# Two-layer graph network: P4 and P5 of each projection made of seven quarter products, inner products first, their weights read from DRAM

## The chip, the core and the metric

The kernel runs on one core of a Trainium2 chip. The metric is the device time of one execution in microseconds; the time before is the median of three runs. The engines are PE (TensorE), DVE (VectorE), ACT (ScalarE), POOL (GpSimd) and SP (SyncE); here SP issues all DMAs.

## The reference

The input x holds 128 graphs of 128 nodes with 512 features, in float32; adj is one 128 x 128 mask. Two layers follow each other, and all products are float32.

```
# layer 0
q, k, v = x @ Wq.T, x @ Wk.T, x @ Wv.T
rel = adj.T * (q @ k.T);  rel = rel / norm(rel, axis=2)
x = layernorm(x + rel @ v)
# layer 1, 8 heads of 64
q, k, v = x @ Wq + bq, x @ Wk + bk, x @ Wv + bv
w = softmax(q @ k.T / 8 + mask(adj))       # per head
x = layernorm(x + (w @ v).merge_heads())
```

## The kernel before

Four graphs make a group g (512 tokens), and there are 32 groups (NG). Layer 0's q and k are folded: M = Wq^T Wk is computed once, and scores are x M x^T. So a group needs five projections of 512 tokens by a 512 x 512 weight: m and v0 of layer 0, and q, k and v1 of layer 1. v0 and v1 come out with tokens on partitions (`wide`), the others with features.

**Seven products.** A projection is a 2 x 2 block product done with seven half-size products instead of eight (Winograd's form of Strassen's method). Product i (P1 to P7) is 256 features by 256 tokens by 256 features: `product(i, bank)` makes it of four matmuls with a moving operand of 256 columns. P1, P6, P7 and P4 add up in one PSUM bank `a` (pool `ps_a`, two banks), which other engines read after each of them. Weight sums are made once (`weight_sums`, kept in `wc`), token sums for each group (`token_sums`, tile `tx`: t0 to t3). In the kernel before, P2 and P3 are not made whole: each is made of seven quarter products of 128 x 128 x 128 (`inner_product`, `inner(o, n)`), with inner weight sums (`wd` and parts of `wc`) and inner token sums (`inner_token_sums`, tile `ux`), in a bank `pc` of the pool `ps_m` (six banks). P1, P5, P6, P7 and P4 are whole. In group 0, m and v0 are `plain`: seven whole products. So is v1 in the last group.

**Order.** The order of all instructions is written out by hand: `at(r, k, f, ...)` puts a step at key 35 r + k, and the kernel emits the steps in order of their keys. Round r holds five projections: m and v0 of group r + 1 at keys 0 and 7, q, k and v1 of group r at 14, 21 and 28. Steps of a projection have keys 0 to 9.74 after its start, so that neighbours interleave. Between them stand the short steps, with keys from the tables ZERO, STEADY, QUICK and LAST. A key of 49 in STEADY means 14 in the next round. Each engine works through its own instructions in this order.

The short steps that matter here, for a group g and a graph b of it:

- `l0_score`: four matmuls, VectorE multiplies with adj (rel), POOL squares it (sq, L500). `l0_norm`: PE sums all four squares (pn, L509), VectorE transposes, POOL takes the power. `l0_out`: one matmul, then three VectorE instructions (L545, L518, L519).
- `attn_scores`: 8 matmuls into two banks, then VectorE's eight masks (L129). `attn_exp`: ScalarE's exponentials in pairs (L583). `attn_spill`, `attn_stage`, `attn_transpose`: the weights go through DRAM, and VectorE transposes them (wT, L602). `attn_out`: 8 matmuls (L615), a VectorE transpose (L618) and a reciprocal. `attn_sum`: one product on VectorE (L644), two sums on POOL (L646, L648). `attn_stats`: VectorE's statistics and four small POOL instructions.
- `x_transpose` and `x1_transpose`: four VectorE transposes for the input of layer 0 and of layer 1; the first half (dh 0) is followed by the token sum t0, the second by t1 (VectorE) and t2, t3 (POOL, L242, L243). Before the change, each transpose of dh 1 is followed by four inner token sums of 128 columns on POOL (L254 to L257).
- `restore`: two POOL copies that put back a weight for the plain v1.

Of the kernel before, what the change touches and what calls it, by code (L numbers as in the profile page):

```python
# [18 lines left out]
def kernel(  # L19
# [29 lines left out]
    small = ctx.enter_context(tc.tile_pool(name="small", bufs=4))  # L49
    dram = ctx.enter_context(tc.tile_pool(name="dram", bufs=2, space=bass.MemoryType.DRAM))  # L50
# [88 lines left out]
    wc = {n: const.tile([P, 7, 2, HF], F32, name=f"wc_{n}") for n in ("m", "v0", "q", "k", "v1")}  # L139


    wd = {n: const.tile([P, 2, 3, P], F32, name=f"wd_{n}") for n in wc}

    def inner_weight(key, o, i):
        if i >= 5:
            return wd[key][:, o - 2, i - 5]
        e, d = {1: (0, 0), 2: (0, 1), 3: (1, 0), 4: (1, 1)}[i]
        return wc[key][:, o - 1, d, e * P:(e + 1) * P]

    kept = const.tile([P, 2, P], F32, name="kept")  # L150

    def restore(key):

        for o in (2, 3):
            nc.gpsimd.tensor_copy(inner_weight(key, o, 3), kept[:, o - 2])

    def inner_weight_sums(key, eng):
        for o in (2, 3):
            w = [None] + [inner_weight(key, o, i) for i in range(1, 8)]
            if key == "v1":  # L160
                eng.tensor_copy(kept[:, o - 2], w[3])
            eng.tensor_tensor(w[5], w[3], w[4], op=ALU.add)
            eng.tensor_tensor(w[6], w[5], w[1], op=ALU.subtract)
            eng.tensor_tensor(w[7], w[1], w[3], op=ALU.subtract)
            eng.tensor_tensor(w[3], w[2], w[6], op=ALU.subtract)

    def weight_sums(t, a21, eng):
        eng.tensor_tensor(t[:, 4], a21, t[:, 3], op=ALU.add)
        eng.tensor_tensor(t[:, 5], t[:, 4], t[:, 0], op=ALU.subtract)
        eng.tensor_tensor(t[:, 6], t[:, 0], a21, op=ALU.subtract)  # L170
        eng.tensor_tensor(t[:, 2], t[:, 1], t[:, 5], op=ALU.subtract)

    def place(t, a21, dc, e, src, copy):

        if dc >= 2:
            dst = t[:, 3 if e else 1, dc - 2]
        else:
            dst = a21[:, dc] if e else t[:, 0, dc]
        copy(dst, src)
# [5 lines left out]

    m21 = two.tile([P, 2, HF], F32, tag="wT", name="m21")
    v21 = two.tile([P, 2, HF], F32, tag="wT", name="v21")

    def layer0_weights():
# [6 lines left out]
        wq_p = one.tile([P, C, C, A, Q], F32, tag="v1", name="wq0_p")  # L196
        for ec in range(C):
            copy = nc.scalar.copy if ec % 2 else nc.vector.tensor_copy
            copy(wq_p[:, ec], quadrants(wq_s[:, ec]))
        for h in range(2):  # L200
            for dh in range(2):
                dst = wc["v0"][:, 3 if h else 1] if dh else v21 if h else wc["v0"][:, 0]
                nc.vector.transpose(dst.rearrange("p c (t s) -> p c t s", s=Q),
                                    wv_s[:, h, :, :, 2 * dh:2 * dh + 2, :].rearrange("p b a c r -> p c (b a) r"))
        x_transpose(0, 0, 0)
        weight_sums(wc["v0"], v21, nc.vector)
        p = [ps_a.tile([P, D], F32, tag="a", name=f"pM_{dc}") if dc < 2 else
             ps_m.tile([P, D], F32, tag="m", name=f"pM_{dc}") for dc in range(C)]
        for ec in range(C):
            for dc in range(C):  # L210
                nc.tensor.matmul(p[dc], wq_p[:, ec, dc].rearrange("p q r -> p (q r)"), quadrants(wk_s[:, ec]),
                                 start=(ec == 0), stop=(ec == C - 1))
        for dc in range(C):
            for e in range(2):
                place(wc["m"], m21, dc, e, p[dc][:, e * HF:(e + 1) * HF], nc.scalar.copy)

    def layer1_weights(name, key):
        w, t = raw[name], wc[key]
        nc.gpsimd.tensor_copy(t[:, 0], w[:, 0:2, 0:HF])
        nc.gpsimd.tensor_copy(t[:, 1], w[:, 2:4, 0:HF])  # L220
        nc.gpsimd.tensor_copy(t[:, 3], w[:, 2:4, HF:D])
        weight_sums(t, w[:, 0:2, HF:D], nc.gpsimd)
# [13 lines left out]
    def token_sums(t, xT, dh, eng=nc.gpsimd):  # L236
# [3 lines left out]
        else:  # L240
            nc.vector.tensor_tensor(t[:, 1], quarter(xT, 1, 1), t[:, 0], op=ALU.subtract)
            nc.gpsimd.tensor_tensor(t[:, 2], quarter(xT, 1, 1), quarter(xT, 0, 1), op=ALU.subtract)  # L242
            nc.gpsimd.tensor_tensor(t[:, 3], quarter(xT, 1, 0), t[:, 1], op=ALU.subtract)  # L243

    def inner_token(xT, o, i):
        d, t = {1: (0, 0), 2: (1, 0), 3: (1, 1), 5: (0, 1)}[i]
        return xT[:, 2 + d, 2 * (o - 2) + t, :]

    def inner_token_sums(u, xT, o):

        b = {i: inner_token(xT, o, i) for i in (1, 2, 3, 5)}
        u = u[:, o - 2]
        eng = nc.gpsimd
        eng.tensor_tensor(u[:, 0], b[5], b[1], op=ALU.subtract)  # L254
        eng.tensor_tensor(u[:, 1], b[3], u[:, 0], op=ALU.subtract)
        eng.tensor_tensor(u[:, 2], b[3], b[5], op=ALU.subtract)
        eng.tensor_tensor(u[:, 3], b[2], u[:, 1], op=ALU.subtract)  # L257

    def x_transpose(g, dh, h):
# [5 lines left out]
        if dh == 1 and h == 0 and g:  # L265
            UX[g] = one.tile([P, 2, 4, P], F32, tag="ux", name=f"ux_{g}")
        transpose_quarter(XT[g], g, h, dh)
        if dh == 1 and g:
            inner_token_sums(UX[g], XT[g], 2 + h)
        if h:  # L270
            token_sums(TX[g], XT[g], dh, nc.gpsimd if g > 1 else nc.vector)
# [11 lines left out]
    def x1_transpose(g, dh, h):  # L283
# [4 lines left out]
        if dh == 1 and h == 0:  # L288
            UX1[g] = one.tile([P, 2, 4, P], F32, tag="ux1" if g < NG - 1 else "ux", name=f"ux1_{g}")
        transpose_quarter(X1T[g], g, h, dh)  # L290
        if dh == 1:
            inner_token_sums(UX1[g], X1T[g], 2 + h)
        if h:
            token_sums(TX1[g], X1T[g], dh)
# [6 lines left out]
    def shared(r):  # L301

        if r not in SX:
            t = one.tile([P, 2, 2, D], F32, tag="yT", name=f"sx_{r}")
            SX[r] = t[:, 0], t[:, 1].rearrange("p s (m e) -> p s m e", m=2)
# [4 lines left out]
    def room(g, b, of):  # L310

        if g >= NG - 2 or (g == NG - 3 and b >= 2):

            i = 2 * b + of if g == NG - 2 else 6 + 2 * b + of
            t = wc["m" if i < 7 else "v0"].rearrange("p i k e -> p (i k e)")
            return t[:, i % 7 * D:(i % 7 + 1) * D]
        if b < 2 and of:
            return shared(g + 1)[0][:, b]
# [8 lines left out]
    class Projection:  # L327


        def __init__(self, kind, g):  # L330
            self.kind, self.g = kind, g
            self.name = f"{kind}_{g}"
            self.w = wc[kind]
            self.wide = kind in ("v0", "v1")

        def begin(self):
            k, g = self.kind, self.g
            x0 = k in ("m", "v0")
            self.xT, self.t = (XT[g], TX[g]) if x0 else (X1T[g], TX1[g])

            self.plain = (x0 and g == 0) or (k == "v1" and g == NG - 1)

            self.late = k == "v1" and g < NG - 1
            if self.late:
                self.s0 = one.tile([P, 2, HF], F32, tag="rel", name=f"s0_{self.name}")
            else:
                self.place()
                self.s0 = self.out(0, 0)

        def place(self):  # L350
            k, g = self.kind, self.g
            if k == "m":
                YT[g] = self.y = one.tile([P, C, G, P], F32, tag="yT", name=f"yT_{g}")
            elif k == "q":
                QT[g] = self.y = one.tile([P, C, G, P], F32, tag="qT" if g < NG - 1 else "yT", name=f"qT_{g}")
            elif k == "k":
                KT[g] = self.y = one.tile([P, C, G, P], F32, tag="kT", name=f"kT_{g}")
            elif k == "v0":
                V0[g] = self.y = one.tile([P, G, D], F32, tag="v0", name=f"v0_{g}")
            else:  # L360
                V1[g] = self.y = one.tile([P, G, D], F32, tag="v1" if g < NG - 1 else "v0", name=f"v1_{g}")

        def out(self, eh, th):
            if self.wide:
                return self.y[:, 2 * th:2 * th + 2, eh * HF:(eh + 1) * HF]
            return quarter(self.y, eh, th)

        def product(self, i, bank, start, within=None):
# [3 lines left out]
            w_ = self.w[:, i - 1]  # L372
            for m in range(2):
                for k in range(2):
# [4 lines left out]
                    if within and m == 0 and k == 0:  # L379
                        within()  # L380

        def empty(self, dst, bank, eh):

            k = self.kind
            if k in ("m", "v0", "v1"):
                nc.scalar.copy(dst, bank)  # L386
            else:
                for m in range(2):
                    nc.scalar.activation(dst[:, m], bank[:, m], AF.Identity,  # L389
                                         bias=b1[k][:, 2 * eh + m:2 * eh + m + 1])  # L390

        def middle(self):

            if self.late:
                s = shared(self.g)[1]
                return s[:, 0], s[:, 1]
            return self.out(0, 1), self.out(1, 1)

        def quarters(self, o, j):

            e, t = j
            y = self.y.rearrange("p a b -> p (a b)" if self.wide else "p c b n -> p (c b n)")
            y = y.rearrange("p (j n) -> p j n", n=P)
# [505 lines left out]
```

## Time and profile before

| | before |
|---|---|
| median of 3 runs | 2438.91 us (2437.82 to 2439.96) |
| profiled execution, its span | 2436.5 us |
| granted TensorE clock, mean | 0.997 |
| PE busy, matmul records | 99%, 16548 |
| DVE, ACT, POOL busy | 76%, 41%, 47% |
| DMA queue of SP | 402.08 MB, 58.9% of 16 engines' span |

The times are those of whole executions, and the span lies between the first and the last instruction of one profiled execution, so a sum of durations is made against the span. A matmul in float32 shows as two records. Busy shares are sums of durations that may overlap by a little when instructions are pipelined. Norm matmuls (pn) of neighbouring groups start at 1266.7 and 1341.0 us, so a round of 35 keys takes 74.3 us and a key about 2.1 us.

### The profile page before, as it was taken

To read this page: it belongs to the slowest core of one execution; us is meant where nothing else is said; L and a number is where in the kernel's file an instruction comes from. 1 tells how busy PE (TensorE), PEld (TensorE's weight loads), DVE (VectorE), ACT (ScalarE), POOL (GpSimd) and SP (SyncE) were. 2 spreads that over 40 slices of the span, in tenths; PEclk is the share of its full clock that TensorE was granted. 3 is DMA by queue.
4 is the path that set the end of the run, shared out by engine and by line. 5 is a ranking of instruction groups with operands and counts; after the bars stand their busy time and mean duration, and the time that the engine had idled before them with its cause. 6 is when DMAs were issued, how large, how long until landed. Compare 5 with 4: busy or idle time off the path is not lost.

```text
span 2436.5 us, 49785 instructions
## 1 busy us (share of the span) xinstructions
PE 2417.1 (99%) x16548; PEld 2131.9 (87%) x16548; DVE 1863.8 (76%) x5934; ACT 1008.7 (41%) x3222; POOL 1138.8 (47%) x1792
## 2 busy tenths in 40 slices
PE   9999999999999999999999999999999999999998
PEld 6888888889888888888898888888888988888886
DVE  5667877777778778777777787787777777877877
ACT  1334343444444343534444443435344444434355
POOL 4624544435535355444455353554444553535543
PEclk9999999999999999999999999999999999999998
DMA  7356556566665665565666556655656665566454
GB/s 161 107 140 175 163 168 183 157 174 169 174 177 160 174 174 165 167 184 156 174 169 175 176 163 171 174 165 167 184 157 173 168 178 175 161 172 175 146 163 138
DMA packets 508611, 405.26 MB, mean 166 GB/s; under 512 B 37568, under 2 KB 424768, under 8 KB 508352
## 3 DMA queue, kind: packets, MB, share of 16 engines
q1 hardware_dynamic: 508352, 402.08, 58.9%
q8 instruction: 129, 2.11, 0.4%
q14 instruction: 130, 1.06, 0.2%
HBM read 237.31 MB, written 164.63 MB: 165 GB/s over the span
## 4 chain that ended last, share of the span: by engine, by line
PE 97%; DVE 1%; DMA 1%; ACT 0%; POOL 0%; issue 0%; SPq 0%; POOLq 0%; DVEq 0%; ACTq 0%
PE pa_v L376 18%; PE pa_q L376 9%; PE pa_m L376 9%; PE pa_k L376 9%; PE pc_v L419 8%; PE ps L563 5%; PE po L615 5%; PE pst L498 5%; PE pb_v L376 5%; PE po L543 4%; PE pc_k L419 4%; PE pc_q L419 4%; PE pc_m L419 4%; PE pb_k L376 2%; PE pb_q L376 2%; PE pb_m L376 2%
## 5 line engine op out<-in xcount | busy, mean ns | idle before, releaser
L523 POOL TENSOR_SCALAR ve<-st 128x1 f32<-128x1 f32 (+1 forms) x157 | 55.8, 356 | 749.2 <-DVE st L519 740.1
L583 ACT ACTIVATE w<-w,nmax 128x128 f32<-128x128 f32 x992 | 384.7, 401 | 4.6 <-DVE nmax L129 4.6
L376 PE MATMUL pa_v<-wc_v,tx 128*128 128x256 f32 x1536 | 368.8, 380 | 0.0
L376 PEld LDWEIGHTS pa_v<-wc_v,tx 128*128 128x128 f32 x1536 | 274.9, 191 | 29.0 <-issue 0.4
L129 DVE CUSTOM_DVE_ANT_0 w<-ps,mask 128x128 f32<-128x128 f32 x1024 | 221.8, 286 | 17.3 <-PE ps L563 15.7
L538 ACT ACTIVATE xr<-xr,sh,rstd 128x512 f32<-128x512 f32 x58 | 47.3, 815 | 401.7 <-POOL sh L533 401.7
L583 ACT ACTIVATION_READ_ACCUMULATOR w<-w,nmax 128x1 f32 x992 | 197.8, 199 | 0.0
L376 PE MATMUL pa_m<-tx,wc_m 128*128 128x256 f32 x768 | 183.8, 382 | 0.9 <-DVE yT L485 0.9
L425 DVE TENSOR_TENSOR v<-pc_v,v 128x256 f32<-128x256 f32 (+1 forms) x434 | 132.0, 309 | 68.4 <-PE pc_v L419 56.7
L376 PEld LDWEIGHTS pa_q<-tx,wc_q 128*128 128x128 f32 x768 | 143.2, 190 | 44.2 <-issue 28.9
L376 PE MATMUL pa_k<-tx,wc_k 128*128 128x256 f32 x768 | 181.8, 380 | 0.0
L376 PE MATMUL pa_q<-tx,wc_q 128*128 128x256 f32 x768 | 181.6, 379 | 0.0
L602 DVE STREAM_TRANSPOSE wT<-wl 128x1024 f32<-128x1024 f32 x124 | 153.4, 1237 | 3.3 <-DMA wl<-wd 3.0
L376 PEld LDWEIGHTS pa_m<-tx,wc_m 128*128 128x128 f32 x768 | 138.6, 190 | 16.4 <-DVE yT L485 1.3
L376 PEld LDWEIGHTS pa_k<-tx,wc_k 128*128 128x128 f32 x768 | 138.4, 190 | 14.9
L425 DVE TENSOR_TENSOR qT<-pc_q,qT 128x128 f32<-128x128 f32 (+1 forms) x320 | 98.4, 315 | 56.9 <-PE pc_q L419 48.4
L389 ACT ACTIVATE qT<-pa_q,bq_sb 128x256 f32<-128x256 f32 x128 | 53.7, 471 | 211.3 <-PE pa_q L376 199.4
L386 ACT COPY yT<-pa_m 128x512 f32<-128x512 f32 x64 | 37.5, 587 | 245.0 <-DVE v L425 112.1
L419 PE MATMUL pc_v<-wd_v,ux 128*128 128x128 f32 x744 | 133.3, 274 | 0.0
L646 POOL TENSOR_TENSOR xr<-xr,bv_b 128x512 f32<-128x512 f32 x58 | 73.8, 1273 | 124.8 <-DMA xr<-x1d 94.8
L563 PE MATMUL ps<-kT,qT 64*128 64x128 f32 x1984 | 130.0, 279 | 0.8 <-DVE nmax L129 0.8
L543 PE MATMUL po<-v,rel 128*128 128x512 f32 x256 | 130.5, 593 | 0.0
(239 smaller groups left out, 6177.8 us busy)
## 6 DMA issues: line engine op xcount, KB each, us to landing
wd<-w SPq DMA_DIRECT2D x248, 256.0 KB, 3.0
wl<-wd SPq DMA_DIRECT2D x496, 128.0 KB, 2.9
xl_x<-in_x_dram SPq DMA_DIRECT2D x256, 128.0 KB, 5.9
x<-in_x_dram SPq DMA_DIRECT2D x64, 512.0 KB, 4.8
x1d<-x SPq DMA_DIRECT2D x64, 512.0 KB, 3.6
xl_h<-x1d SPq DMA_DIRECT2D x256, 128.0 KB, 2.8
od<-oT SPq DMA_DIRECT2D x496, 64.0 KB, 2.1
o<-od SPq DMA_DIRECT2D x118, 256.0 KB, 2.9
```

Source lines behind the costliest of these rows:

```text
L129: nc.vector.tensor_tensor_reduce(out=dst, in0=scores, in1=m, scale=-HD ** -0.5, scalar=3.0e38, op0=ALU.add, op1=ALU.min, accum_out=least)
L376: nc.tensor.matmul(bank[:, m, :], l[:, k, m * P:(m + 1) * P], r[:, k, :], start=start and m == 0 and k == 0, stop=(m == 1 and k == 1), ski ...
L419: nc.tensor.matmul(self.c[o][:, slot, :], l, r, start=start, stop=True, skip_group_check=True)
L425: nc.vector.tensor_tensor(y, self.c[o][:, slot], s if kept else y, op=ALU.add)
L498: nc.tensor.matmul(p, XT[g][:, dc, b, :], YT[g][:, dc, b, :], start=(dc == 0), stop=(dc == C - 1))
L523: nc.gpsimd.tensor_scalar(ve[:, :n], stats[:, :n, 1], EPS, None, op0=ALU.add)
L543: nc.tensor.matmul(p, REL[g][0][:, b, :], V0[g][:, b, :], start=True, stop=True)
L563: nc.tensor.matmul(p[s][:, :, a, :], QT[g][r, a, b, :], KT[g][r, a, b, :], start=True, stop=True)
L583: nc.scalar.activation(w[:, s, :, a, :], w[:, s, :, a, :], AF.Exp, bias=nmax[:, i:i + 1], scale=-1.0, accum_out=sums[:, i:i + 1])
L602: nc.vector.transpose(wT, SOFT[g, b][0].rearrange("p a i r -> p i a r"))
L615: nc.tensor.matmul(p[s * HD:(s + 1) * HD, a, :], V1[g][:, b, h * HD:(h + 1) * HD], wT[:, s * (H // 2) + a].rearrange("p q t -> p (q t)"), ...
L646: nc.gpsimd.tensor_tensor(xr, xr, bv_b, op=ALU.add)
```

## The change

P4 and P5 of every projection that isn't plain are now made of seven quarter products as well, so only P1, P6 and P7 are whole. v1 of the last group is no longer plain, and `restore` is gone.

- **Inner products.** `inner(th, n)` makes two inner projections at once: P2 with P4 for th = 0, P3 with P5 for th = 1. Each pair of matmuls writes neighbouring parts of one bank. For n = 0 to 2 it issues four matmuls of 128 columns, for n = 3 two. ScalarE copies the partial results out of the bank after n = 0 (one copy), n = 1 (two) and n = 3 (one); VectorE adds after n = 0 and n = 2. After n = 3 of th = 1 a new POOL instruction adds P3's and P5's parts (512 columns).
- **Whole products.** `whole(i, m)` makes half of a whole product (two matmuls); VectorE adds the bank to the output after each half of P1 and P6, and twice after P7. The bias of q and k is added there, by `scalar_tensor_tensor`.
- **Order.** Inner steps come first: keys 0 to 3.5 for th = 0, 2.4 to 5.83 for th = 1; the halves of P1, P6 and P7 at 4.17, 5.33, 6.5, 7.67, 8.83 and 10.0. Some keys of the tables move by up to 1.5 (32 to 32.75 for attn_scores, 10.5 to 11.5 for l0_score and so on).
- **Token sums.** The inner sums run on two blocks at a time (256 columns), all after the last transpose: t1 (VectorE), t3 (POOL), four sums of raw tokens, four of summed tokens, then t2. `ux` grows from 8 to 14 blocks.
- **Weights.** The parts for P4 and P5 (`WDR`, 7 KB a partition) are written to DRAM once, and `stream(kind, g)` reads them into a ring of two buffers for each projection, 7.5 keys before its start.

```diff
-    wc = {n: const.tile([P, 7, 2, HF], F32, name=f"wc_{n}") for n in ("m", "v0", "q", "k", "v1")}
+    wc = {n: const.tile([P, 5, 2, HF], F32, name=f"wc_{n}") for n in KINDS}
+    def stream(key, g):
+        WR[key, g] = ring.tile([P, 2, 7, P], F32, tag="wr", name=f"wr_{key}_{g}")
+        nc.sync.dma_start(WR[key, g], WDR[key])
...
+    def token_sums(t, xT, u, dh, eng=nc.gpsimd):
         if dh == 0:
             eng.tensor_tensor(t[:, 0], quarter(xT, 0, 1), quarter(xT, 0, 0), op=ALU.subtract)
-        else:
-            nc.vector.tensor_tensor(t[:, 1], quarter(xT, 1, 1), t[:, 0], op=ALU.subtract)
-            nc.gpsimd.tensor_tensor(t[:, 2], quarter(xT, 1, 1), quarter(xT, 0, 1), op=ALU.subtract)
-            nc.gpsimd.tensor_tensor(t[:, 3], quarter(xT, 1, 0), t[:, 1], op=ALU.subtract)
+            return
+        nc.vector.tensor_tensor(t[:, 1], quarter(xT, 1, 1), t[:, 0], op=ALU.subtract)
+        nc.gpsimd.tensor_tensor(t[:, 3], quarter(xT, 1, 0), t[:, 1], op=ALU.subtract)
+        if u is not None:
+            inner_token_sums([None] + [raw_token(xT, i) for i in (1, 2, 3)] + [None, raw_token(xT, 5)],
+                             [u[:, j:j + 5:4] for j in range(4)])
+            r = [None] + [sum_token(t, i) for i in (1, 2, 3)] + [None, sum_token(t, 5)]
+            inner_token_sums(r, [u[:, 8:12:3], u[:, 9:13:3], r[5], u[:, 10:14:3]])
+        nc.gpsimd.tensor_tensor(t[:, 2], quarter(xT, 1, 1), quarter(xT, 0, 1), op=ALU.subtract)
...
+        def inner(self, th, n):
+            if n == 0 and th == 0:
+                self.begin()
+            y = self.blocks(th)
+            if n == 0:
+                self.c[th] = c = ps_m.tile([P, 2, 2, P], F32, tag="m", name=f"pc{th}_{self.name}")
+                d = ps_m.tile([P, 2, P], F32, tag="m", name=f"pd{th}_{self.name}")
+                self.inner_products(th, 1, c[:, 1], True)
+                self.inner_products(th, 2, d, True)
+                nc.scalar.copy(y[:, 0, 0], c[:, 1])
+                nc.vector.tensor_tensor(y[:, 0, 0], d, y[:, 0, 0], op=ALU.add)
+            elif n == 1:
+                c = self.c[th]
+                self.inner_products(th, 6, c[:, 1])
+                self.inner_products(th, 5, c[:, 0])
+                nc.scalar.copy(y[:, 1, 0], c[:, 1])
+                nc.scalar.copy(y[:, 1, 1], c[:, 0])
+            elif n == 2:
+                c = self.c[th]
+                self.inner_products(th, 7, c[:, 1])
+                self.inner_products(th, 3, c[:, 0])
+                nc.vector.tensor_tensor(y[:, 1], c, y[:, 1], op=ALU.add)
             else:
+                c = self.c[th]
+                self.inner_products(th, 4, c[:, 1])
+                nc.scalar.copy(y[:, 0, 1], c[:, 1])
+                if th:
+                    nc.gpsimd.tensor_tensor(self.held(0, 1), self.held(0, 1), self.held(1, 1), op=ALU.add)
...
+        def whole(self, i, m):
+            if i == 1 and m == 0:
+                self.a = ps_a.tile([P, 2, HF], F32, tag="a", name=f"pa_{self.name}")
...
+            self.product(i, self.a, i == 1, (m,))
+            if i == 1:
+                self.add(0, 0, (m,))
+            elif i == 6:
+                self.add(0, 1, (m,))
+            elif m == 1:
+                self.add(1, 0)
+                self.add(1, 1)
...
+    WHOLES = ((4.17, 1, 0), (5.33, 1, 1), (6.5, 6, 0), (7.67, 6, 1), (8.83, 7, 0), (10.0, 7, 1))
+    INNER = ((0, 0, 0), (1.17, 0, 1), (2.33, 0, 2), (3.5, 0, 3), (2.4, 1, 0), (3.57, 1, 1), (4.67, 1, 2), (5.83, 1, 3))
```

Keys of ZERO and STEADY that the prediction speaks of, after the change: l0_score at 11.5, 11.5, 11.75 and 12.5, l0_norm at 13.75, x1_transpose at 2.5, 3.5, 6 and 9.5 of a round, x_transpose at 25.5, 27, 28.5 and 30, attn_out and attn_scores at 14 (graphs 0, 1 out; 2, 3 scored) and at 32.75 (2, 3 out; 0, 1 of the next group scored), attn_stats of graph 3 at 12, attn_sum of graphs 0 and 1 at 25, all exponentials of graph 3 at 20.

## The prediction

> **What bounds the kernel now.** I read the page's busy times and slices first, then the chain that ended last.
>
> ```profile
> PE 2417.1 (99%) x16548; PEld 2131.9 (87%) x16548; DVE 1863.8 (76%) x5934; ACT 1008.7 (41%) x3222; POOL 1138.8 (47%) x1792
> ...
> PE   9999999999999999999999999999999999999998
> ...
> PE 97%; DVE 1%; DMA 1%; ACT 0%; POOL 0%; issue 0%; SPq 0%; POOLq 0%; DVEq 0%; ACTq 0%
> ```
>
> TensorE works in every slice and carries 97% of the chain. The list of PE's waits says how little is lost elsewhere (us in total, times, longest):
>
> ```profile
> PE po L615 <- DVE wT L602: 3.1, 2, 2.5
> PE pz L195 <- POOL zeros L192: 1.2, 1, 1.2
> ...
> PE pn L509 <- POOL sq L500: 0.9, 1, 0.9
> ```
>
> All its lines add up to 13 us. So fewer matmul cycles are time saved, and any new wait of PE is time lost. Prices of PE come from the chain in order of time, where pieces follow each other without gaps (start, us, records):
>
> ```profile
> 1008.47 1.90 PE po L615 x32
> 1010.37 1.99 PE ps L563 x32
> ...
> 1023.25 1.73 PE pa_m L376 x8
> 1024.98 1.11 PE pc_m L419 x10
> ...
> 1043.22 0.36 PE pn L509 x8
> ```
>
> A matmul is two records. 256 columns: 1.73/8 = 0.216 us a record; 128 columns: 1.11/10 = 0.111. One steady round is five projections, each 20 wide and 14 narrow matmuls: 40 x 0.2165 + 28 x 0.1113 = 11.78, x5 = 58.9; plus four of attn_out (0.95), attn_scores (1.0), l0_score (0.89), l0_out (0.86) and the norm matmul (0.36): 15.2. Sum 74.1; the norm matmuls at 1266.7 and 1341.0 lie 74.3 apart. Nothing else is in a round.
>
> **How the engines hand over.** The Trainium skill, "TensorE: Matmul & The Clock Gate", on the architecture of the array, says that matmuls keep program order and that the queues of ScalarE, VectorE and GpSimd are strict FIFO. The trace agrees as far as it shows: an instruction whose input is ready starts only after the one before it. "PSUM — Partial Sum Buffer", on bank collisions, asks that accesses be guarded by bank and not by address. The kernel before does it: `last_out` writes the second head's columns (L716) of a bank while VectorE reads the first's (L721), and PE starts 0.06 us after that read ends:
>
> ```profile
> 2416.42 0.42 DVE L721 TENSOR_TENSOR o<-po,rs 128x256 f32<-128x256 f32 x1 [0.26 <-PE po L716]
> ...
> 2416.90 1.10 PE L716 MATMUL po<-v,wT 128*128 128x64 f32 x8
> ```
>
> So I count a wait for every new product into a bank that another engine still reads, other columns included.
>
> **Part 1, the products.** P4 and P5 lose 8 wide matmuls and gain 14 narrow ones: 16 x 0.2165 - 28 x 0.1113 = 0.35 us per projection. With 157 such projections, and v1 of the last group from seven wide products (12.12) to the new form (11.43), PE saves 55 us. A round falls to 5 x 11.43 + 15.2 = 72.35 us.
>
> **Part 2, the order.** Before, a whole product (1.73) ran between hand-overs, and keys of successive uses of bank a were 3 apart (6 us). Now wholes come in halves (0.87) 1.17 keys apart with mostly one inner step (0.89) between; bank a is handed over by VectorE four times a projection, each inner bank by ScalarE or VectorE three times. The cover is about 0.9 us. VectorE's work in a round is nearly the same (per projection 14 adds before, 10 or 12 wider ones now), but it stands in bursts.
>
> **Part 3, POOL.** The eight inner token sums of x1 (and of x) double in width, and all of them now stand behind the transpose of the second half; before, four of them ran earlier. POOL's groups by shape (busy us, mean ns of one, idle before):
>
> ```profile
> L242 POOL TENSOR_TENSOR tx<-x1T 128x512 f32<-128x512 f32 x32 | 40.6, 1268 | 0.0
> ...
> L256 POOL TENSOR_TENSOR ux<-x1T 128x128 f32<-128x128 f32 x64 | 29.0, 454 | 0.0
> ```
>
> And POOL's instructions in order of time (start, duration in us):
>
> ```profile
> 1037.54 1.27 POOL L242 TENSOR_TENSOR tx<-x1T 128x512 f32<-128x512 f32 x1
> 1038.77 1.27 POOL L243 TENSOR_TENSOR tx<-x1T,tx 128x512 f32<-128x512 f32 x1
> 1039.99 1.12 POOL L500 TENSOR_TENSOR sq<-rel 128x128 f32<-128x128 f32 x3
> 1041.90 0.40 POOL L500 TENSOR_TENSOR sq<-rel 128x128 f32<-128x128 f32 x1 [0.79 <-DVE rel L499]
> ```
>
> The last square ends at 1042.3, PE needs it at 1043.22: 0.9 us of slack. A 256-wide sum has no row. Between the two shapes above POOL pays 2.12 ns a column ("GPSIMD Engine Reference", elementwise accounting: 2.6 cycles at 1.2 GHz, 2.17 ns, agrees), so 0.73 us; bounds 0.62 and 0.85. Added too: a 512-wide add (1.27) in every projection, between ScalarE's last copy and VectorE's add of P6. While VectorE waits for it, everything in its queue waits: the adds that hand banks back to PE, l0_out, the masks.
>
> **The sum, by walking a round.** Clock 0 is the norm matmul. I lay each engine's instructions in program order, each starting when its queue and its inputs allow. Prices from the rows: VectorE 0.34 a 256-wide add, 0.58 a 512-wide one, 1.62 an l0_out, 1.7 the masks of one graph, 1.15 a wT; ScalarE 0.3 to 0.4 a copy, 0.385 an exponential; POOL as above.
>
> Three waits in full. (a) **Norm matmul.** From key 9.5, x1_transpose(1,1), VectorE needs 1.7 us (its backlog 0.4, the transpose 0.6, the sum t1 0.65) to what POOL waits for. Then POOL: t3 1.25, eight sums 5.8, t2 1.25, three squares 1.2, attn_stats of graph 3 (1.46, now ahead of the last square) and that square 0.4: 13.1. PE's work from there: whole halves and inner steps 6.15, four scores 3.56: 9.7. Wait **3.3**, after rounding. (b) **v1's P6.** Before, the masks ended 6.4 us after attn_out began (1008.5 to 1014.9); P1's second-half add stands behind them, done at 6.75. PE: 1.9 + 2.0 + 0.87 + 0.45 = 5.2. Wait **1.5**. (c) **v0's P7**, the same burst at key 14: add 7.6 after attn_out, PE 6.55. Wait **1.05**.
>
> The rest of the walk (PE there, released, cause):
>
> | step | there | free | cause |
> |---|---|---|---|
> | k inner 1 | 21.0 | 21.4 | copy behind graph 3's eight exponentials |
> | q P7 | 23.15 | 23.8 | add behind l0_out |
> | k P1, 2nd half | 30.4 | 31.05 | add behind attn_sum's two products |
> | k inner (1,3) | 31.9 | 32.25 | add behind an x transpose |
> | k P6, 2nd half | 34.45 | 35.55 | POOL's new add behind four attn_sum ops |
> | k P7 | 37.3 | 38.0 | add behind wT and x transpose |
> | m P6 | 62.7 | 63.3 | add behind statistics |
> | m P6, 2nd half | 65.05 | 66.1 | POOL's new add behind statistics |
>
> These are 5.4 us; with (a) to (c) 11.25. A round takes 72.35 + 11.25 = 83.6, 9.2 more than 74.4. It repeats in 30 rounds: +276. The 55 us are in that, but for the first and last rounds, where I set 2 us of saving against some 20 added setup sums of POOL (0.46 each, half hidden): +3. The profiled execution's 2436.5 and the 2.4 to the median of 2438.9: 2718. Nearly half of the waits are below 1 us and hang on single durations, so I take 2700.
>
> **Edits costed at nothing.** 157 streams of 0.92 MB go onto SP's queue (402 MB become 546, share 59% to about 80% at most). A 512 KB load lands in 4.8 us, so 9.6 is a ceiling for one; each is issued 7.5 keys, 15 us, ahead, and waits only for PE's inner steps that end 0.7 key before. SP behind it holds stagings whose transposes come over 5 us later. "DMA: Bandwidth & Descriptors", measured bandwidth, has 1 MB at 6.15 us, which agrees. If that cover is gone, each late stream costs PE its lateness, at most some 3 us. The removed restore and the keys shifted by up to one unit (2.1 us) cost nothing by themselves. After a wait PE's first product also shows its weight load (1.94 to 2.01 for 1.73 in the first rounds): up to 0.2 for each of eleven, +66 at the top of the range; below nothing they can't go.
>
> **Rivals.**
> Faster: *VectorE and POOL keep up.* If the waits stay below 1.83 us a round (55/30) the saved cycles win; with none, 2384. For it: before, the same engines caused 13 us in all. Against: (a) alone is 3.3 and needs no assumption on banks. It decides with POOL: at 0.46 a sum, as if width cost nothing, (a) falls to 1.1.
> Slower, small: *only the POOL chain and the mask bursts hold*, the bank hand-overs being looser than the L716 row suggests: 72.35 + 5.85 = 78.2, +3.8 a round, 2555; with (a) alone 2478.
> Slower, more: *streams collide with stagings*, 3 us in each of 30 rounds on top: 2790.
> *The change doesn't do what it says*: PE would not show 16548 + 157 x 12 + 24 = 18456 matmul records, nor the DMA list 157 streams.
>
> **How the numbers follow.** A measurement tells about 0.2% (4.9 us) from no change. The walk with its small waits 0.55 (2600 to 2800, predicted 2700); only the large waits 0.17 (2450 to 2600); streams on top 0.08 (to 2850); waits below the saving 0.20 (2384 to 2444), of which 0.02 within 0.2%. The range, 2395 to 2810, leaves out the lowest part of the last case and the top of the streams. Faster 0.18, same 0.02, slower 0.80.
>
> **What would show it.** PE's waits: pn on POOL sq some 90 to 110 us in all, P6 and P7 (pa tiles) on VectorE over 100; PE's busy share near 90%; POOL near 60%; the distance between norm matmuls about 83 us. Wrong if that distance is below 74.4, if pn doesn't wait, or if PE waits for the streamed tiles.

## The result and the profile after

The changed kernel takes 3177.99 us (median, 3165.2 to 3184.7) against 2439.43 of the kernel before: ratio 1.302, 95% interval 1.299 to 1.305. The direction was forecast; the size was not: 2700 was predicted, 2810 was the top of the range.

The page of the changed kernel: span, busy time and instructions, and PE's busy tenths in 40 slices.

```profile
span 3181.8 us, 54401 instructions
...
PE 2638.7 (83%) x18456; PEld 2262.9 (71%) x18456; DVE 1927.3 (61%) x5440; ACT 1020.3 (32%) x3598; POOL 1467.6 (46%) x1958
...
PE   7888888888888888888888888888888888888887
```

The 18456 matmul records are there, so the change does what it says. (Of the streams the program issues 156 in its rounds and two more loads of that size in the setup; the prediction counted 157.) But PE is busy for 83% only, and no other engine is above 61%: nothing has become the bound by its amount of work. POOL stands at 46%, not near 60%: its 1468 us would be 54% even of the predicted 2718. Even PE's busy time has grown, from 2417 to 2639 us, although it has fewer cycles of work. A matmul that takes longer than before is the first sign of something beside waits. The page's chain is of no help this time:

```profile
PE 0%; DVE 0%; POOL 0%; issue 0%; POOLq 0%; DVEq 0%
```

It could be followed back over the last 30 us only, so its shares say nothing of the rounds. The distance of the norm matmuls does: in the trace they start at 1275.14, 1371.56 and 1470.22, 96.4 and 98.7 us apart (74.3 before, 83.6 predicted).

PE's list of waits (us in total, times, longest) came to 13 us before. In its names `pa` is bank a, `pc` and `pd` are the banks of the inner steps, the letter behind is the projection, and v stands for v0 and v1 alike:

```profile
PE pc_v L446 <- ACT v L458: 144.4, 30, 6.7
PE pn L553 <- POOL sq L544: 104.9, 31, 3.5
PE pa_k L436 <- DVE kT L483: 88.3, 89, 2.0
PE pa_v L436 <- DVE v L491: 70.6, 64, 8.1
PE pa_m L436 <- DVE yT L491: 61.8, 73, 2.0
PE pa_q L436 <- DVE qT L483: 13.7, 31, 1.3
```

Lines two to six were predicted: pn on POOL at 105 (forecast 90 to 110), the pa tiles on VectorE at 234 (forecast over 100). The first line was not. The same list for two rounds, from one norm matmul to the one two rounds later:

```profile
PE pn L553 <- POOL sq L544: 10.5, 3, 3.5
PE pc_v L446 <- ACT v L458: 10.0, 2, 5.5
PE pa_k L436 <- DVE kT L483: 5.8, 6, 1.3
PE pa_m L436 <- DVE yT L491: 4.2, 5, 1.6
PE pa_v L436 <- DVE v L491: 3.9, 4, 1.5
PE pa_q L436 <- DVE qT L483: 0.8, 2, 0.4
PE pc_k L446 <- ACT kT L458: 0.6, 2, 0.3
PE pc_m L446 <- ACT yT L458: 0.4, 2, 0.2
```

One of the three pn lies on the edge and does not count. Per round that is 5.0 us of waiting for v0's first copy and 11.4 us for everything else. The walk had 11.25, all of it in this second part.

**Where v0 waits.** ScalarE's instructions in order of time (start, duration, in brackets the idle time before and its releaser):

```profile
1344.20 0.39 ACT L627 ACTIVATE w<-w,nmax 128x128 f32<-128x128 f32 x1
1344.49 0.19 ACT L627 ACTIVATION_READ_ACCUMULATOR w<-w,nmax 128x1 f32 x1
1345.30 0.81 ACT L582 ACTIVATE xr<-xr,sh,rstd 128x512 f32<-128x512 f32 x1 [0.61 <-POOL sh L577]
1352.23 0.37 ACT L458 COPY v<-pc_v 128x256 f32<-128x256 f32 x1 [6.12 <-DMA wd<-w]
```

and SP's queue in the same stretch:

```profile
1342.76 0.32 SPq L193 DMA_DIRECT2D wr_q<-wr_q  x1
1343.19 1.90 SPq L642 DMA_DIRECT2D wl<-wd  x4
1345.13 1.21 SPq L634 DMA_DIRECT2D wd<-w  x2
```

v0's output tile lives in the slot "v0", which the attention weights w of graphs 0 and 1 hold until their spill (wd<-w) has landed. The spill of graph 1 stands at key 6.5; v0's first write now comes with the first inner step at key 7, and the second inner step, at 8.17, needs the bank that this copy empties. Before, a whole product of 1.73 us stood ahead of the first write and the bank was not wanted again for three keys. At key 6.5 the program issues q's stream first (0.9 MB), then the staging of graph 0, then the spill. The last exponential ended about 1344.7, the spill was issued from 1345.13, and landed by 1352.2. PE stood for 4.53 us.

**What follows a long wait.** PE in order of time behind v0's wait, and behind the norm matmul's:

```profile
1352.66 0.80 PE L446 MATMUL pc_v<-wd_v,ux 128*128 128x128 f32 x2 [4.53 <-ACT v L458]
1353.25 0.64 PE L446 MATMUL pc_v<-wr_v,ux 128*128 128x128 f32 x2
...
1354.53 1.91 PE L436 MATMUL pa_m<-tx,wc_m 128*128 128x256 f32 x4
...
1371.56 0.66 PE L553 MATMUL pn<-sq,ones 128*32 128x128 f32 x8 [3.49 <-POOL sq L544]
1372.14 3.68 PE L659 MATMUL po<-wT,v 128*64 128x128 f32 x32
```

From start to start attn_out takes 3.6 us, 1.90 before, and a half of P7 1.71 instead of 0.87. The table by stretches has the reason (window, its length, busy time and instructions of PE, PEld, DVE, ACT, POOL, then the granted clock, DMA share, GB/s):

```profile
1352.70:1357.00 4.30, 4.30 (x18) 3.94 (x19) 1.84 (x3) 0.65 (x2) 0.00 (x0) 0.55 0.25 74
1357.00:1360.00 3.00, 3.00 (x26) 2.90 (x25) 2.19 (x4) 0.66 (x2) 0.00 (x0) 1.00 0.81 255
1371.60:1378.30 6.70, 6.70 (x72) 5.91 (x72) 3.08 (x13) 0.40 (x1) 2.16 (x2) 0.59 0.18 58
1379.00:1382.00 3.00, 2.51 (x18) 2.22 (x17) 2.70 (x22) 1.84 (x8) 0.00 (x0) 1.00 0.27 24
```

Behind both waits PE ran at about half clock. The Trainium skill, "TensorE: Matmul & The Clock Gate", part 1, says that the array's clock is halved after at least one idle window of about 3.4 us and restored after a busy window of that length. These traces agree in part: waits of 3.5 and 4.5 us were followed by half clock, those of 1.5 us here were not. But a wait need not be as long as that window. In a run below (both cures) half clock also follows waits of 1.9 and 2.2 us; a pair takes 0.43 from start to start there, in place of 0.22:

```profile
1362.82 0.49 PE L446 MATMUL pc_q<-x1T,wc_q 128*128 128x128 f32 x2 [2.24 <-DVE oT L662]
...
1365.70 0.63 PE L446 MATMUL pc_q<-ux,wd_q 128*128 128x128 f32 x2
```

Start to start, attn_out and attn_scores lost 6.2 - 3.9 = 2.3 us, and the six pieces behind v0's wait 4.0 - 2.0 = 2.0.

**One round accounted for.** Mean of the two rounds from 1275.14 to 1470.22, each piece's start-to-start time less its price at full clock:

| part | predicted | measured |
|---|---|---|
| PE's own work | 72.35 | 72 |
| waits of the walk | 11.25 | 11.4 |
| v0's first copy | 0 | 5.0 |
| half clock | 0 | about 4.2 |
| entering and leaving waits, weight loads laid bare | 0 | about 4.9 |
| round | 83.6 | 97.5 |

The last two rows together are what is left over, 9.1; the experiments split them. The kernel before has 0.8 left over.

Not all of the 745 us between the two spans lies in the 30 steady rounds. From the second norm matmul to the last it is 700 (2227.8 us before, 2927.7 after); 45 stand in the first and last rounds, for which the prediction had 3. Two single waits in the first round, of 8.5 and 8.1 us (pc_m for an x transpose, pa_v for VectorE), are part of it; the rest was not followed.

### The profile page after: what moved, and what is told of

Read it like the earlier page. It is cut to its first block, busy times and chain, and to the rows that moved or that the text cites. A ratio compares the mean times of both kernels' runs of the same rounds, so it can differ in the third digit from the quotient of the medians.

```text
span 3181.8 us, 54401 instructions
## 1 busy us (share of the span) xinstructions
PE 2638.7 (83%) x18456; PEld 2262.9 (71%) x18456; DVE 1927.3 (61%) x5440; ACT 1020.3 (32%) x3598; POOL 1467.6 (46%) x1958
## 5 line engine op out<-in xcount | busy, mean ns | idle before, releaser
L436 PE MATMUL pa_v<-wc_v,tx 128*128 128x256 f32 x1024 | 270.4, 387 | 61.6 <-DVE v L491 61.5
L446 PE MATMUL pc_v<-wd_v,ux 128*128 128x128 f32 x756 | 176.0, 320 | 144.4 <-ACT v L458 144.4
L476 POOL TENSOR_TENSOR qT<-qT 128x512 f32<-128x512 f32 x32 | 40.6, 1269 | 523.0 <-ACT qT L474 523.0
L446 PEld LDWEIGHTS pc_v<-wd_v,ux 128*128 128x128 f32 x756 | 143.6, 223 | 174.6 <-ACT v L458 156.4
L436 PEld LDWEIGHTS pa_v<-wc_v,tx 128*128 128x128 f32 x1024 | 175.3, 191 | 87.7 <-DVE v L491 73.8
L491 DVE TENSOR_TENSOR v<-pa_v,v 128x256 f32<-128x256 f32 x190 | 79.2, 417 | 178.3 <-POOL v L476 150.6
L659 PE MATMUL po<-wT,v 128*64 128x128 f32 x1984 | 167.7, 339 | 3.5 <-DVE wT L646 3.5
L659 PEld LDWEIGHTS po<-wT,v 128*64 128x64 f32 x1984 | 149.1, 176 | 19.6 <-issue 15.9
L446 PE MATMUL pc_v<-wr_v,ux 128*128 128x128 f32 x756 | 161.0, 298 | 0.0
L483 DVE SCALAR_TENSOR_TENSOR kT<-pa_k,bk_sb,kT 128x256 f32<-128x256 f32 x256 | 113.5, 475 | 74.3 <-POOL kT L476 68.8
L446 PE MATMUL pc_v<-wr_v,tx 128*128 128x128 f32 x756 | 154.5, 288 | 0.0
```

The source lines that it names most:

```text
L436: nc.tensor.matmul(bank[:, m, :], l[:, k, m * P:(m + 1) * P], r[:, k, :], start=start and m == 0 and k == 0, stop=(m == 1 and k == 1), ski ...
L446: nc.tensor.matmul(dst[:, n, :], l, r, start=start and n == 0, stop=True, skip_group_check=True)
L476: nc.gpsimd.tensor_tensor(self.held(0, 1), self.held(0, 1), self.held(1, 1), op=ALU.add)
L483: nc.vector.scalar_tensor_tensor(o, self.a[:, m], b1[self.kind][:, 2 * eh + m:2 * eh + m + 1], o, op0=ALU.add, op1=ALU.add)
L491: nc.vector.tensor_tensor(o[:, m], self.a[:, m], s[:, m], op=ALU.add)
L659: nc.tensor.matmul(p[s * HD:(s + 1) * HD, a, :], V1[g][b // 2][:, b % 2, h * HD:(h + 1) * HD], wT[:, s * (H // 2) + a].rearrange("p q t -> ...
```

## The experiments

Each is one run on the chip, unless said otherwise. The changed kernel's own runs lie within 20 us of each other, so no smaller difference is read as a gain.

### Is it the half clock? Fill two waits with idle work

```diff
+ for i in range(15):                       # in l0_norm, ahead of pn's own products
+     nc.tensor.matmul(pn[...], ident, wc["q"][:, 0, 0, :P], start=True, stop=True)
+ for i in range(10):                       # in v0, ahead of the products of inner(0, 1)
+     nc.tensor.matmul(self.a[:, 0], ident, wc["q"][:, 0, 0], start=True, stop=True)
```

> Nothing is taken away; PE gets idle work in two waits of the changed kernel: 15 matmuls of 128 columns into pn before each norm matmul (about 3.3 us), and 10 of 256 columns into v0's fresh bank a before v0's second inner step (about 4.3 us). Their results are overwritten. Theory A (a wait of 3.5 us or more costs its length again or more, because TensorE runs at half clock for some us after it): the two waits fall below 1 us each, their length being filled, the mean granted clock rises from 0.93 to 0.98 or more, and the time falls by 100 to 215 us, to 2960 to 3080. Theory B (the clock record has nothing to do with these waits, or half clock there costs nothing): 3180 or more, the clock stays near 0.93.

3071.3 us, clock 0.989 (changed kernel: 0.933). PE does 765 matmuls more (1530 records) and the kernel is 107 us faster. The two waits in the list of this run:

```profile
PE pc_v L446 <- ACT v L458: 21.6, 24, 2.2
PE pn L560 <- POOL sq L548: 8.6, 26, 4.5
```

No wait was shortened, PE was only kept busy in it. So half clock is a cost of its own, as theory A said, at the low end of its gain. The left-over of a round, counted in the same way, fell from 9.1 to 5.0 us: 4.1 us of half clock, in accord with the 4.3 read off the pieces. (In 30 rounds that would be 123 us; the idle matmuls take some 0.5 us a round more than the waits that they replace.)

### Is it the stream ahead of the spill? Issue the streams 0.1 key later

```diff
-                    at(r, 7 * j - 7.5, stream, kind, g)
+                    at(r, 7 * j - 7.4, stream, kind, g)
```

> The five streams are issued 0.1 key later, so that on SP's queue the staging of b0 and the spill of b1 go ahead of q's stream. Theory A (the stream in front of the spill is what makes its landing late): spill of b1 issued 0.4 us earlier and landed in 4 us instead of 6, v0's first copy waits 2 to 3 us less per round, and with the half clock behind it 80 to 150 us go: 3030 to 3100. Theory B (the spill comes too late for v0's first write whatever stands ahead of it; transfers share the same 16 engines anyway): 3150 to 3185.

2987.8 us. Repeated in three rounds:

> The streams 0.1 key later, timed in three rounds: if the gain of some 190 us on the changed kernel is the edit's and not the run's, 2970 to 3005, ratio to the kernel before 1.22 to 1.23. If it was a stray run, nearer 3178.

2976.8 us, ratio 1.221 (1.219 to 1.224): some 200 us for the order of issues on one queue, more than theory A had. The list of DMA issues (engine, count, KB each, median us from issue to landing), of the changed kernel:

```profile
wd<-w SPq DMA_DIRECT2D x248, 256.0 KB, 5.2
...
wr_q<-wr_q SPq DMA_DIRECT2D x32, 896.0 KB, 5.0
```

and with the streams later:

```profile
wd<-w SPq DMA_DIRECT2D x248, 256.0 KB, 3.7
...
wr_q<-wr_q SPq DMA_DIRECT2D x32, 896.0 KB, 5.6
```

The spills land 1.5 us sooner, q's stream 0.6 us later, and nothing in PE's list waits for it. v0's wait falls from 144 to 17 us, and the clock record's loss (time at half clock, halved) from 216 to 108 us.

### What do the streams cost in all? Leave them out

```diff
-        WR[key, g] = ring.tile([P, 2, 7, P], F32, tag="wr", ...)
-        nc.sync.dma_start(WR[key, g], WDR[key])
+        WR[key, g] = WR["m", 0]
```

> The changed kernel without the 157 streams: all projections take P4's and P5's weights from one tile that is loaded in the setup, so the values of P4 and P5 are not those of the reference; the number and the form of all other instructions stay. Theory A (the whole price of the streams is that q's stands ahead of the spill that frees v0's slot): as the run with the streams 0.1 key later, 2988, give or take 15; v0's wait below 20 us, pn's wait still 105. Theory B (the traffic itself costs, on the engines of the DMA, all round): below 2950. Theory C (the spill is late without them too): above 3100.

2951.3 us: 227 us less than the changed kernel, 26 to 37 less than with the streams in their better place. 2951.3 is between theories A and B, at the edge of B: nearly nine tenths of the streams' price is their place in the queue, a small rest is traffic.

### Take the norm matmul's wait away

```diff
-        ((11.5, 11.5, 11.75, 12.5), 13.75, ...
+        ((11.5, 11.5, 11.75, 12.5), 16.2, ...
-                      two.tile([P, G, P], F32, tag="oT", name=f"sq_{g}"))
+            t = one.tile([P, 2, G, P], F32, tag="rel", ...); REL[g] = t[:, 0], t[:, 1]
```

> The norm matmul goes from key 13.75 to 16.2; so that it can stand behind attn_out, its squares move from the slot of oT to the unused half of the slot of rel. Theory A (the wait of pn for POOL's sums costs its 3.4 us a round and about as much again in half clock behind it): pn's 105 us fall to below 10, time falls by 170 to 220 us to 2960 to 3010. Theory B (waits alone, no clock): 105 us less, 3075. Theory C (the late queue of POOL then shows elsewhere, at l0_out or at the adds that wait for POOL): 3150 or more.

3129.6 us, 48 less, where 105 us of wait alone had been expected to go and 170 to 220 with the clock. Two lines of its list of waits say why:

```profile
PE pc_v L446 <- ACT v L458: 148.3, 30, 6.6
...
PE pc_q L446 <- DVE oT L662: 56.2, 30, 2.3
```

pn's wait is gone, and q's first inner step now waits for a bank that VectorE's transpose of attn_out still reads. The trace of one round has the reason (VectorE, VectorE, PE):

```profile
1155.75 0.42 DVE L491 TENSOR_TENSOR v<-pa_v,v 128x256 f32<-128x256 f32 x1 [4.84 <-POOL v L476]
1156.10 0.70 DVE L662 STREAM_TRANSPOSE oT<-po 128x512 f32<-128x512 f32 x1
...
1156.86 0.49 PE L446 MATMUL pc_q<-x1T,wc_q 128*128 128x128 f32 x2 [1.90 <-DVE oT L662]
```

VectorE itself has stood 4.84 us for POOL's new add of v0, with the transpose behind it in its queue. In the changed kernel VectorE stands at this place as long, beside pn's wait, and PE is not held up by it:

```profile
1372.77 0.42 DVE L491 TENSOR_TENSOR v<-pa_v,v 128x256 f32<-128x256 f32 x1 [4.98 <-POOL v L476]
```

So POOL's late queue shows at the next place, as theory C had it, though the time lies between the ranges of B and C. Half of the 105 us came back as this wait. v0's wait is untouched.

### Both cures

```diff
-        (32.75, (35.5, 38.5, 38.5, 41.5, 41.5), (41.5, 41.5), 42, ...
+        (32.75, (35.5, 38.5, 38.5, 39.75, 39.75), (39.75, 39.75), 42, ...
```

> As the run before, and in addition the last two pairs of exponentials of graph 1 and its spill go from key 41.5 to 39.75, ahead of q's stream. Theory A (two places, v0's slot and the norm matmul, with the half clock behind each, are what the prediction had too low): v0's wait for the spill is below 20 us in all, clock above 0.98, and the time is the predicted walk without its largest wait: 72.35 + 8 + some 2.2 us of weight loads a round, 2650 to 2730. Theory B (the hand-over of banks costs far more than the walk has, and these waits only stood in front of it): 2850 or more.

This is the late norm matmul with another cure for v0's slot: the spill earlier, not the streams later. 2947.1 us, clock 0.977, a round 89.2. v0's wait for the spill is gone and pn's is 2 us in all. Theory B: with both places cured the time is still 217 us above the top of what the walk without its largest wait would give. The pa tiles wait 250 us in all here, 234 in the changed kernel, and pc_q 64.

### What do the hand-overs hang on?

**A bank for each half of the whole products** (three banks for a, five for the inner steps).

```diff
-                self.a = ps_a.tile([P, 2, HF], F32, tag="a", ...)
+                self.a.append(ps_a.tile([P, HF], F32, tag="a", name=f"pa{m}_{self.name}"))
```

> On top of the run with norm matmul and spill moved (2947): each half of the whole products gets a bank of its own (bank a becomes two of three banks, the inner steps' pool shrinks from six to five), and P7's adds go by halves. The products and the adds' elements are the same. Theory A (PE waits for VectorE because the two halves share a bank; with a bank each, a half has the other half and two inner steps, some 2.6 us more, as cover): PE's waits on the pa tiles, 250 us there, fall below 100, and with 0.27 us of drain and refill per wait that goes some 200 us: 2720 to 2790. Theory B (VectorE and POOL are late by more than any cover, their queues set the pace): waits on pa tiles stay above 200, 2900 to 2960. Theory C (five banks are too few for the inner steps): new waits on pc and pd tiles, above 2960.

2996.6 us, 50 more than without. The waits on pa tiles fell from 250 to 3 us, which bears out that the halves were held up by the bank they share. But the time did not fall; PE now waits here:

```profile
PE pc_v L447 <- DVE v L471: 128.4, 57, 8.1
PE ps L609 <- DVE oT L664: 81.4, 29, 2.9
PE pc_m L447 <- ACT yT L459: 58.5, 30, 2.0
PE pc_k L447 <- DVE kT L471: 40.5, 30, 2.8
```

The time is in theory C's range, and that theory blames the five banks. Whether they are too few, or the readers are as late as before and PE only meets them at another tile, this run can't tell, since it changes both pools; a run below that keeps six banks speaks for the second.

**The scores of two graphs no longer together**, so that VectorE's masks come in four bursts.

```diff
-        (32.75, (35.5, 38.5, ...
+        (33.9, (35.5, 38.5, ...
-        (49, (49.5, 49.5, ...
+        (48.25, (49.5, 49.5, ...
```

> On top of the run with norm matmul and spill moved (2947): the attention scores of two graphs no longer stand together; graph 1's go from key 32.75 to 33.9 and graph 2's from 49 to 48.25, so that their masks, 1.7 us a graph on VectorE, come in four bursts and not in two. Theory A (the bursts stand in front of the adds that hand bank a back): waits on pa tiles and of pc_q for oT fall from 310 to 200 us, 2810 to 2870. Theory B (the waits follow from the 0.9 us of cover, whatever the order of VectorE's work): 2920 to 2960.

2873.6 us, 73 less than both cures alone, just above the range of theory A; yet the pa tiles still wait 244 us, so its reason, bursts ahead of the adds of bank a, is not borne out. What went is the new wait of pc_q for oT (64 us) with what hangs on it.

> Own banks for the halves and spread scores together, on top of 2947. Theory A (both hold): 2620 to 2720. If only one of them holds, as the better of the two runs before, within 20 us.

With the banks too: 2846.8. Neither range: the two together are 27 us better than spreading alone, and far from the sum that theory A had.

**VectorE does the add of L476 in place of POOL.**

```diff
-                    nc.gpsimd.tensor_tensor(self.held(0, 1), self.held(0, 1), self.held(1, 1), op=ALU.add)
+                    nc.vector.tensor_tensor(self.held(0, 1), self.held(0, 1), self.held(1, 1), op=ALU.add)
```

> The changed kernel with one edit: the 512-wide add before P6's add (L476) is done by VectorE (0.68 us) and not by POOL (1.27). Theory A (this new add stands behind POOL's attn_sum, statistics and token sums, and VectorE's queue stands behind it; this is where k's, m's and v1's late adds come from): VectorE's idle time for POOL at P6, 280 us there, goes; waits of PE on pa tiles fall from 234 to 130 us or less, pn's wait falls by 1.2 us a round since two adds less stand ahead of the squares, and the time by 100 to 180 us: 3000 to 3080. Theory B (the late adds come from VectorE's own queue, masks, transposes, attn_sum's product; POOL's add is just what VectorE is seen to wait for): 3140 to 3200.

In the changed kernel, as its only edit: 3212.1, 34 us slower, beyond both ranges. PE's list again:

```profile
PE pc_v L446 <- ACT v L458: 178.9, 30, 7.0
PE pn L553 <- POOL sq L544: 121.2, 32, 4.1
```

The pa tiles' waits fell by 39 us (234 to 195), but these two grew by 51. At v0's slot PE comes sooner and stands longer: counted from the norm matmul (median of the rounds) it is there after 72.9 us, 73.9 without the edit, and goes on after 78.9, 78.8 without it. So a gain ahead of this place can't show while its wait is set by a DMA. At the norm matmul PE comes no sooner, 16.0 us after v0's release for 15.9; there the squares are 0.7 us later, and no run shows why.

> The same edit on top of spread scores, early spill and late norm matmul (2874). Theory A: 2740 to 2800, waits on pa tiles 244 us there, below 120. Theory B: 2850 to 2890.

The same edit behind the cures and the spread scores: 2785.8, 88 us faster than without, and the pa tiles' waits fall from 244 to 148. Theory A, in its range for the time; the waits were to fall below 120.

> The same edit with a bank for each half (2847 without it). Theory A: the inner banks' waits on VectorE's adds of pc, 170 us there, fall below 80, since VectorE no longer stands behind POOL; 2700 to 2770. Theory B: 2830 to 2870.

With a bank for each half: 2795.9, 51 faster than without the edit; the inner banks' waits on VectorE's adds of pc fell only from 171 to 150. Between the theories.

**Whole products uncut**, inner steps put in another order, streams issued still later: three edits at once.

> On top of 2786 (late norm matmul, early spill, spread scores, VectorE's add): the whole products P1, P6 and P7 are no longer cut in halves, so bank a is handed over twice inside a projection and not four times, with 1.8 to 2.7 us of inner steps between; the inner steps are put in such an order that between two uses of an inner bank there stands other work; the streams are issued 0.6 key later. Products and weights are the same. Theory A (the change's order, 0.87 us of cover at every hand-over, is what makes PE wait, bank by bank): PE's waits on pa tiles, 147 us there, fall below 50 and those on pc tiles stay below 60; 2560 to 2660. Theory B (VectorE's queue is late by as much as any order gives): 2740 to 2800.

2839.3, 54 slower than the 2785.8 it starts from. The pa tiles' waits fall to 27 us, and pc_v and pc_k take them over:

```profile
PE pc_v L446 <- DVE v L470: 127.4, 62, 2.9
PE pc_k L446 <- DVE kT L470: 65.1, 62, 4.0
```

That is slower than either range, on the side of theory B. As in the run with a bank for each half, the waits on bank a went nearly to nothing and came back on the inner steps' banks, here with all six of them.

### What is left

> As the run of 2786, but the spill keeps its key 41.5 and the streams are issued 0.1 key later, so that q's stands behind staging and spill. Theory A (the early spill delayed the stagings that VectorE's transposes need, 117 us of VectorE's idle time there, and the adds behind them): VectorE waits for wl below 20 us, time 2700 to 2750. Theory B (those waits of VectorE lie beside other work): 2770 to 2800.

This is the run of 2785.8 with the streams later in place of the spill earlier. 2792.2, the same within the scatter. VectorE's idle time for wl fell from 117 to 11 us and the time did not move: it lay beside other work (theory B).

> The run before without the 157 streams (P4's and P5's weights from one tile loaded in the setup, so the values of P4 and P5 are not the reference's). Theory A (the traffic has little left to cost once its place in the queue is right): 5 to 25 us less than the run before. Theory B (half of the rest hangs on the traffic): over 100 us less.

2745.8, 46 less: again neither end. With the queue in order, the traffic of the streams costs about 46 us.

> As the first run of this group, and attn_sum of graph 1 goes from key 60 to 62, so that two products of VectorE (1.28 us) and four adds of POOL no longer stand together in k. Theory A (k's waits on pa, 83 us, come from this burst): 40 to 80 us less than the first. Theory B (another burst takes its place): within 20 us of it.

2769.9, and in three rounds:

> All cures that helped, timed in three rounds: 2755 to 2795, ratio 1.13 to 1.145; the edit of attn_sum alone (22 us against the run without it) may be within the scatter.

2770.0, ratio 1.136 (1.134 to 1.139). k's waits on pa fell from 85 to 63 us (69 in the repeat), which fits the 22 us; as a difference of time that is just about the scatter, and it lies between the two ranges. This is the fastest version found that has its streams. No version beat the kernel before.

A round takes 83.6 us in it (mean of two, from 1291.11 to 1458.25 us), PE's own work 72.3. Of the 11.3 between them the recorded waits are only 5.4. The other 5.9 lie beside the waits, and the clock record has no half clock there; about half of them stand directly before and behind a wait and may go with it. Without these waits a round would still take 78.2 us, or some 75 if that half went too: more than the 74.3 of the kernel before, which has less than 1 us of such losses.

## Why the prediction was wrong, step by step

- **The products (part 1): right.** PE's work in a round is 72 us by its pieces, against 72.35.
- **The order and POOL (parts 2 and 3, the walk): right in mechanism, and in its sum by some luck.** pn waits 3.5 us (predicted 3.3), v1's P6 1.49 (1.5), k's P1 1.07 (0.65), k's P6 1.33 (1.1), k's P7 0.42 (0.7), q's P7 0.41 (0.65), m's P6 0.68 and 1.56 (0.6 and 1.05), k's inner 1 0.32 (0.4), v0's P7 0.48 (1.05). k's inner (1,3) has no wait in the list; m's second inner step has one, 0.22. The total of 11.4 for 11.25 is closer than the single terms, which are off by up to 0.6 us in both directions. (The eight terms of the table add up to 5.5, not 5.4.) The estimate of 0.73 us for a 256-wide sum on POOL was met: 0.73 in the trace.
- **"Edits costed at nothing", the streams: the step that failed first.** I asked what the streams' own readers would feel, and what SP holds behind them for the transposes. I did not list what the spill behind q's stream releases: the slot that v0's output shares with w. And part 2 moved v0's first write ahead of the whole product that had covered it, which the walk took as free. It measures 5.0 us a round as a wait, and with the half clock behind it the place of the stream is worth some 200 us.
- **Waits charged at their length only: the second.** pn's 3.3 us was predicted as 3.3. Behind it and behind v0's wait TensorE runs at half clock, 4.1 us a round, 107 us in the run that filled the waits. A predicted wait of 3.3 us was long enough to ask for this. The prediction has no term for it.
- **"After a wait PE's first product also shows its weight load": mis-sized.** It was put at nothing, at most 0.2 us for each of eleven. All that lies beside the recorded waits comes to about 4.9 us a round, by the left-over of the run with filled waits. Of it, 2.1 stand ahead of the dozen waits that the list shows (m's P6 lost 1.72 for a recorded 1.56), which the prediction did not price. About 1.2 stand at the first products behind them, some 0.1 each, within its 0.2. The rest, again about 0.1 us each, stands at a dozen places without a wait in the list, at products whose first weight load comes late. That these are hand-overs released just in time is read from the traces and was not tried.
- **The first and last rounds: mis-sized.** 3 us were set for them; they cost 45.
- **The rivals.** "Streams collide with stagings" (2790) named the right queue and the wrong transfer. "VectorE and POOL keep up" fell with the first list of waits. "Only the POOL chain and the mask bursts" fell too: the hand-overs of banks wait as the L716 row had suggested, and giving the halves banks of their own took just those waits away.
- **Chance.** The fastest version's round takes the predicted 83.6 us, but not for the predicted reason: 11.25 of them were to be waits, and 5.4 are.
- **Open.** What would end the remaining waits, and the losses beside them. Two different layouts moved the waits from bank a to the inner steps' banks, and moving POOL's add helped; this fits readers whose queues are late wherever PE meets them. No run removed that lateness itself.

## What to carry to other kernels

When a write moves forward, look up which tile held its slot before, what releases that tile, and what stands ahead of the release on its queue; a DMA that nobody waits for today can be the one that frees a slot tomorrow. Price a wait of TensorE by its length class: in these traces 1.5 us costs itself and a few tenths, 3.5 us or more costs itself and about 2 us of half clock behind it, and waits of 1.9 and 2.2 us had half clock behind them in some rounds. If such a wait can't be removed, idle matmuls can be tried in it; here they gave 3.4%. With several waits in a round, cure the one set by the slowest chain first: VectorE's add measured 34 us slower before the cures and 88 us faster behind them. And when a wait is cured, look at what stood idle beside it, since that can be the next wait.

## What the runs showed of the hardware that was not expected

- Half clock, in the clock's record, comes in stretches of 3.4 us and multiples (67 of 68 in the changed kernel, 48 of them 6.83): 431 us of the changed kernel's span, 15.6 us of the kernel before. The record alone overstates the loss: part of such a stretch lies over the wait itself. Filling the waits took the record's loss from 216 to 34 us, but only 107 us from the time.
- Adding 765 matmuls whose results are overwritten made the kernel 3.4% faster.
- A 512 KB spill of x (x1d<-x) takes 6.5 us to land in the changed kernel and 2.8 in the run without streams; the 896 KB streams themselves take 4.5 to 5.6.
